# Attention and top-1 experts on one Trainium2 core: the first group's tokens are finished in their places and scattered straight to the output

## The chip, the cores and the metric

One core of a Trainium2 chip. The time is the device time of one execution in microseconds (us), the median of several runs; lower is better. The engines are TensorE (PE; its weight loads are listed apart as PEld), VectorE (DVE), ScalarE (ACT), GpSimd (POOL) and SyncE (SP), which here only issues DMA transfers. The kernel is written with a fixed order: what the code emits for an engine runs on that engine in the emitted order, and the transfers of SP's queue likewise.

## The reference

```
x = x + LN(attn(LN(x)))                     # (2, 2048, 256), 4 heads of 64
x = x + LN(ffn(LN(x)))

attn:  xn = LN(x)*gamma + beta;  q, k, v = xn @ w.T, split in heads
       q, k = rmsnorm(q, q_gamma) * 64**-0.5, rmsnorm(k, k_gamma)
       softmax(q k^T) v, heads joined, @ w_o.T + b_o

ffn:   chosen = argmax(x @ gate_w.T)        # one of 8 experts for each token
       return x + expert_w[chosen] @ x
```

All in float32. LN without gamma and beta is the plain layer norm over the 256 columns. So each token needs attention over its batch's 2048 tokens, and then one 256x256 product with the weight of the expert that the gate chose for it.

## The kernel before

**Tokens and steps.** The 4096 tokens are 32 tiles of 128, 16 to a batch. Attention is a row of 256 steps, taken two by two as 128 pairs; below, a slot is the work of one pair. For each step, `scores` makes s = K·Qᵀ on PE (L1071, for two heads and 512 queries) and ACT turns it into p = exp(s) (L1079, five buffers of p, two PSUM tiles of s); `add` sums p over the keys on DVE (L1112, L1114), `weigh` multiplies by V on PE into po (L1123). In a slot the code emits the scores of the next pair, the sums of this pair, then `between(now)`, and then the po of this pair. `between` moves every running generator on by one step: all other work (projections, tokens, gate, places) is made of generators whose steps it puts into the slots. After the last pair `finish` runs what is left, each time the step that can start first by costs written in the code.

**Tokens after attention.** When four tiles have their attention, `tokens` (L811) makes for each: py = oT·woT on PE (L817), y = py + bias (L832) with the gate's columns, the norm's moments on DVE (L387, L389), rs and shift on POOL (`norm`: rs L383, shift L400; here they are named rs_z and away), then x2 = y·scale + xr (L843), the gate's scores into the group's `picks` (L851), the moments of x2, and x2n = LN(x2) on ACT (L868). SP writes x2 (L871) and x2n (L872) to DRAM, 128 KB each.

**Groups.** Tiles 0 to 15 are group A (T=16), tiles 16 to 27 group B (T=12); the last four tiles go a dense way with all eight experts. When the last tile of a group has its scores, `choose_all` (L580, last instruction L593) finds the expert of each token on DVE, and `order` (L597) sorts the tokens by expert into S = T+7 places of 128 rows, so that each place holds tokens of one expert: two rank matmuls on PE (L603, L604), a chain of small DVE instructions that ends in each token's position `pos` (L652), then, a slot later, the place's expert, and the matrices ids (L678, L679) and inrow (L686, four 128x512 instructions), and two slots later a product on PE (src, L696, one 128x128 by S matmul for each of the T tiles) that gives for each place the list of its tokens. DVE casts it to integers (L703).

**Places.** One place begins in each slot. `places` (L717): POOL gathers the 128 rows of x2n by src (L722, into one of six row buffers), SP loads the expert's weight (L736), PE transposes the rows (pt_g, L744), ACT copies them (xT, L749), PE multiplies (pe, L754), ACT copies out (f, L764), DVE makes the moments, POOL rs_f and shift_f (L383, L400), ACT the norm (L770), and SP writes f as 128 rows of `fn` (L771).

**Collection.** When all places of a group are written, `collect` (L781) gathers for each tile its tokens' rows of fn by pos on POOL (L792), reads x2 back on SP (L800), adds both and `away` on DVE (L804) and writes the tile of the output on SP (L808). `away` is the part of x2 that was kept aside (minus the mean times the scale). For group A this comes among the last pairs of attention, 622 to 710 us, beside the tokens and the gate of group B.

The lines that decide where the source product stands:

```
            yield
            yield
            ps = ps_m(f"src{n}")
            for t in range(T):
                nc.tensor.matmul(ps[:, :S], inrow[t // QT4][:, t % QT4, :],
                    ids[:, t, :], start=(t == 0), stop=(t == T - 1))
            nc.vector.tensor_copy(gr.src, ps[:, :S])
            at = now + 1
            for j in range(S):
                at += 0.34 if at >= len(steps) // PAIR + lead else 1
```

Of the kernel before, what the change touches and what calls it, by code (L numbers as in the profile page):

```python
# [9 lines left out]
F32 = mybir.dt.float32  # L10
# [10 lines left out]
GAMMA_MAX = 5.0  # L21
RAISE = 1 / 16


@with_exitstack
def kernel(
# [95 lines left out]
    bo = const.tile([P, D], F32, tag="bo", name="bo")  # L122
    nc.gpsimd.dma_start(out=bo, in_=b_o.partition_broadcast(P))
# [51 lines left out]

    DG = D + E
# [4 lines left out]
    bias_o = const.tile([P, DG], F32, tag="bias_o", name="bias_o")  # L181

# [44 lines left out]
    def turn_outputs(w, ps, turned):  # L227
# [26 lines left out]
        for c in range(NCH):  # L254
# [6 lines left out]
            )  # L261
        nc.gpsimd.tensor_copy(bias_o[:, :D], bo)
        nc.vector.tensor_copy(bias_o[:, D:], pb[:, :E])
# [18 lines left out]
    def bounded_path():  # L282
# [55 lines left out]
        def tables():  # L338


            make_upper_triangular(nc, before, 1.0, diag=False)
            nc.gpsimd.memset(allones, 1.0)
            for r, step, per_partition in ((col, 1, 0), (col128, P, 0), (token, P, 1)):
                nc.gpsimd.iota(
                    r,
                    [[step, r.shape[-1]]],
                    base=0,
                    channel_multiplier=per_partition,
                    allow_small_or_imprecise_dtypes=True,
                )  # L350
            yield
# [179 lines left out]
        ring = []  # L531
        rows = []
        spare = []

        def more_room():

            for i in range(2):
                acc = wk.tile([P, HP, KB], F32, tag="acc", name=f"rows{i}", bufs=2)
                rows.extend(acc[:, r, i : i + D] for r in range(HP) for i in range(0, KB, D))
            p = wk.tile([P, HP, KB], F32, tag="p", name="spare", bufs=5)  # L540
            spare.extend(p[:, r, i : i + D] for r in range(HP) for i in range(0, KB, D))
            have["f"] += len(spare)
            KT = batches[-1].KT
            ring.extend(
                KT[:, c, i : i + NCH * D].rearrange("p (c d) -> p c d", d=D)
                for c in range(NCH)
                for i in range(0, N, NCH * D)
            )

        def load_experts():  # L550
# [5 lines left out]
            )  # L556
            xg = wk.tile([P, 6, D], F32, tag="rows", name="rows", bufs=1)
            rows.extend(xg[:, i, :] for i in range(6))
            weD = kv.tile([P, NCH, E, D], F32, tag="KT", name="weD")
# [4 lines left out]
        class Group:  # L564


            def __init__(self, name, n):
# [4 lines left out]
                self.pos = route.tile([P, n], U32, tag=f"pos{name}", name=f"pos{name}")  # L572
                self.src = route.tile([P, self.S], U32, tag=f"src{name}", name=f"src{name}")
                self.exp = route.tile([P, self.S], I32, tag=f"exp{name}", name=f"exp{name}")
                self.away = route.tile([P, n], F32, tag=f"away{name}", name=f"away{name}")
                rows = dict(x2=n * P, x2n=n * P, fn=self.S * P)
                for k, v in rows.items():
                    setattr(self, k, dram.tile([v, D], F32, tag=k + name, name=k + name))

# [17 lines left out]
        def order(gr):  # L597
# [53 lines left out]
            nc.vector.tensor_reduce(pos, w, AX.X, ALU.add)  # L651
            nc.vector.tensor_copy(gr.pos, pos)  # L652
            yield
# [38 lines left out]
            yield  # L692
            yield
            ps = ps_m(f"src{n}")
            for t in range(T):
# [6 lines left out]
                )  # L702
            nc.vector.tensor_copy(gr.src, ps[:, :S])  # L703

            at = now + 1
            for j in range(S):
                at += 0.34 if at >= len(steps) // PAIR + lead else 1
                g = opens(early(places(gr, j)), Next("POOL", 1.3), 0, lambda: 0.0 if ring and rows else None)
                queue.append((at, g))
            for t in range(T):  # L710
                at += 0.5 if at >= len(steps) // PAIR + lead else 1
# [4 lines left out]

        def places(gr, j):  # L717

            n = f"{gr.name}{j}"
# [29 lines left out]
            nc.scalar.copy(xT, pt[:, :D].rearrange("p (c n) -> p c n", n=P))  # L749
            rows.append(xg)  # L750
            yield later("PE", 0.9, take="mf", give="m")
            pe = ps_m(f"pe{n}")[:, :D]
# [4 lines left out]
            ring.append(w)  # L757
            f = spare.pop() if spare else None
            own = f is None
            if own:  # L760
                f = wk.tile([P, D], F32, tag="fl", name=f"f{n}", bufs=5)
            yield then("ACT", 1.5 if j % 3 == 0 else 0.4, give="x")
# [12 lines left out]
            if not own:  # L775
                spare.append(f)
            yield later("", 0.0, give="f")
# [3 lines left out]
        def collect(gr, t):  # L781

            n = f"{gr.name}{t}"
            if attending:
                z = wk.tile([P, 2 * D], F32, tag="fg", name=f"fg{n}")
            else:
                if not free:
                    qt = kv.tile([P, NCH, KB], F32, tag="QT", name=f"fg{n}", bufs=NKB + 1)
                    free.extend(qt[:, c, :] for c in range(NCH))
                z = free.pop(0)  # L790
            o, x2 = z[:, :D], z[:, D:]
# [9 lines left out]
            yield later("DVE", 0.5, 3.0)  # L801
            if attending:
                yield later("DVE", 0.5)
            nc.vector.scalar_tensor_tensor(  # L804
# [6 lines left out]
        def tokens(bt, qb, j, oTs, gr):  # L811
# [21 lines left out]
            nc.sync.dma_start(out=xr, in_=x_f[tt * P : (tt + 1) * P, :])  # L833
            if gr:
                away = gr.away[:, tt - gr.first : tt - gr.first + 1]
# [96 lines left out]

        have = dict(m=3, s=2, x=4, f=4)

# [620 lines left out]
```

## Time and profile before

| what | us |
|---|---|
| median of three runs (802.62, 804.57, 805.9) | 804.57 |
| the profiled execution | 796.33 |
| its span (first to last instruction) | 794.6 |
| PE busy | 760.0 |
| DVE / ACT / POOL busy | 607.9 / 459.6 / 323.9 |
| L792, 16 gathers of A's collection on POOL | 18.2 |
| L804, 16 adds of A's collection on DVE | 7.7 |
| L722, 23 gathers of A's places on POOL | 28.9 |
| pairs of attention with A's places among them | 495 to 600 |
| B's gate, from the last picks on | 678 on |
| end of attention | 717 |

"Span" is the profiled time on the chip; the mean granted clock of PE over it was 0.982. In the lines of the profile "out<-in" names the tiles, "x" counts, and what stands in square brackets is the idle time of the engine just before, with what ended it. The transfers of A's fn took 2.5 us from issue to landing, those of x2 1.7, of the weights (ring) 2.9, all by SP's queue.

### The profile page before, as it was taken

Reading aid. Unit: us, or ns where it says so; the run is one execution under the profiler, and the core shown is the slowest. Engines: PE = TensorE matmul, PEld = TensorE weight load, DVE = VectorE, ACT = ScalarE, POOL = GpSimd, SP = SyncE. Lnnn points to the kernel's source line nnn. Section 1 sums busy time; section 2 is a strip of 40 time slices with the busy share of each in tenths; the row PEclk is TensorE's granted clock in tenths of the full one; section 3 lists DMA queues with packets and bytes.
Section 4 is the critical chain, followed back from the end, with each engine's and each line's share of the span. In section 5 each row is a group of like instructions: output and inputs, shape, how many; then the busy total and the mean of one; then the engine's idle time right before and its main releaser. Section 6 shows DMA issues by size and latency. Waiting matters only on the chain.

```text
span 794.6 us, 10249 instructions
## 1 busy us (share of the span) xinstructions
PE 760.0 (96%) x3169; PEld 320.3 (40%) x3169; DVE 607.9 (77%) x1239; ACT 459.6 (58%) x725; POOL 323.9 (41%) x349
## 2 busy tenths in 40 slices
PE   7999999999999999999999989999999999898794
PEld 5555433433343334333333343444444333335452
DVE  3666567598886877887888986777786889996767
ACT  3766765656565566556556525566656555445861
POOL 4644311133342523432325121757663455335324
PEclk9999999999999999999999979999999999899998
DMA  4100121210110000000221040443421243358336
GB/s 129 55 27 26 41 80 40 67 34 19 35 34 7 21 21 20 21 21 20 73 81 47 27 132 14 127 132 110 112 66 34 80 120 99 124 155 255 90 114 188
DMA packets 48149, 57.57 MB, mean 72 GB/s; under 512 B 5868, under 2 KB 39416, under 8 KB 48088
## 3 DMA queue, kind: packets, MB, share of 16 engines
q1 hardware_dynamic: 41528, 44.65, 17.8%
q0 software_dynamic: 3568, 9.32, 4.7%
q10 hardware_dynamic: 2992, 2.88, 1.3%
q8 instruction: 27, 0.44, 0.3%
q14 instruction: 34, 0.28, 0.1%
HBM read 37.69 MB, written 19.14 MB: 72 GB/s over the span
## 4 chain that ended last, share of the span: by engine, by line
PE 85%; DVE 8%; ACT 3%; issue 2%; POOL 2%; DMA 1%; POOLq 0%; DVEq 0%; ACTq 0%
PE s L1071 28%; PE po L1123 27%; PE pqk L464 7%; PE pv L473 4%; PE py L817 3%; PE peA L754 3%; PE pe L893 2%; PE pt_qk L501 2%; PE sm L1087 2%; DVE acc L1114 2%; PE pt_x L451 1%; PE peB L754 1%; DVE acc L1099 1%; PE srcA L696 1%; PE pt_gA L744 1%
## 5 line engine op out<-in xcount | busy, mean ns | idle before, releaser
L1079 ACT ACTIVATE p<-s,nbound 128x1024 f32<-128x1024 f32 x256 | 271.4, 1110 | 232.2 <-PE s L1071 224.5
L1114 DVE TENSOR_TENSOR acc<-acc,p 128x1024 f32<-128x1024 f32 x224 | 273.8, 1222 | 37.0 <-ACT p L1079 25.5
L1071 PE MATMUL s<-QT,KT 64*128 64x512 f32 x1024 | 256.5, 619 | 0.4 <-ACT p L1079 0.4
L1123 PE MATMUL po<-p,V 128*64 128x512 f32 x1024 | 251.6, 613 | 0.0
L1071 PEld LDWEIGHTS s<-QT,KT 64*128 64x128 f32 x1024 | 89.0, 188 | 164.6 <-issue 96.1
L1123 PEld LDWEIGHTS po<-p,V 128*64 128x64 f32 x1024 | 64.1, 137 | 129.8 <-issue 127.3
L383 POOL TENSOR_TENSOR rs_z<-rs_t,mhalf 128x1 f32<-128x1 f32 x28 | 36.8, 1316 | 123.3 <-DVE rs_t L382 123.2
L383 POOL TENSOR_TENSOR rn<-rs_t,mhalf 128x8 f32<-128x8 f32 x32 | 58.6, 1831 | 69.3 <-DVE rs_t L382 69.3
L464 PE MATMUL pqk<-wqkT,xnT 128*128 128x512 f32 x128 | 62.4, 611 | 0.6 <-ACT xnT L455 0.6
L383 POOL TENSOR_TENSOR roots<-rs_t,mhalf 128x1 f32<-128x1 f32 x32 | 23.9, 747 | 93.3 <-DVE rs_t L382 93.1
L1099 DVE RECIPROCAL acc<-acc 128x128 f32<-128x128 f32 x60 | 56.7, 945 | 0.0
L383 POOL TENSOR_TENSOR rs_y<-rs_t,mhalf 128x1 f32<-128x1 f32 x28 | 33.7, 1204 | 35.4 <-DVE rs_t L382 32.8
L832 DVE TENSOR_TENSOR y<-py,bias_o 128x264 f32<-128x264 f32 x28 | 12.0, 430 | 41.8 <-PE py L817 41.8
L722 POOL DMA_INDIRECT rows<-x2nA,srcA x23 | 28.9, 1257 | 30.1 <-DMA ring<-weTd 24.7
L817 PE MATMUL py<-woT,oT 128*128 128x264 f32 x128 | 35.7, 402 | 3.6 <-ACT xTB L749 2.3
L792 POOL DMA_INDIRECT fgA<-fnA,posA x16 | 18.2, 1136 | 44.8 <-DMA out_dram<-fgA 10.3
L473 PE MATMUL pv<-wvT,xnT 128*128 128x264 f32 x128 | 33.7, 386 | 0.0
L487 DVE TENSOR_REDUCE ss<-sq 128x8 f32<-128x512 f32 x32 | 21.8, 680 | 14.9 <-ACT sq L484 14.9
L473 PEld LDWEIGHTS pv<-wvT,xnT 128*128 128x128 f32 x128 | 24.5, 191 | 17.8 <-issue 10.4
L817 PEld LDWEIGHTS py<-woT,oT 128*128 128x128 f32 x128 | 22.0, 189 | 18.9 <-issue 12.1
L464 PEld LDWEIGHTS pqk<-wqkT,xnT 128*128 128x128 f32 x128 | 22.3, 195 | 17.7 <-issue 16.6
L481 ACT COPY qk<-pqk 128x512 f32<-128x512 f32 x32 | 18.7, 585 | 17.6 <-PE pqk L464 17.4
(270 smaller groups left out, 882.1 us busy)
## 6 DMA issues: line engine op xcount, KB each, us to landing
ring<-weTd SPq DMA_DIRECT2D x34, 256.0 KB, 2.9
x<-in_L_attn_x_dram SPq DMA_DIRECT2D x8, 512.0 KB, 3.9
xr<-in_L_attn_x_dram SPq DMA_DIRECT2D x28, 128.0 KB, 2.3
fnA<-fA SPq DMA_DIRECT2D x23, 128.0 KB, 2.5
we_raw<-in_L_ffn_expert_w_dram ACTq DMA_DIRECT2D x8, 256.0 KB, 2.7
weTd<-weT SPq DMA_DIRECT2D x8, 256.0 KB, 2.0
x2A<-x SPq DMA_DIRECT2D x16, 128.0 KB, 1.7
fgA<-x2A SPq DMA_DIRECT2D x16, 128.0 KB, 2.0
```

Of the source, the lines that this page charges most:

```text
L383: nc.gpsimd.tensor_tensor(dst, t[:, :n], mhalf[:, :n], ALU.pow)
L464: nc.tensor.matmul(pqk, xnT[:, c, :], wqkT[:, c, :, :].rearrange("p a d -> p (a d)"), start=(c == 0), stop=(c == NCH - 1),)
L473: nc.tensor.matmul(pv[:, :DG], xnT[:, c, :], wvT[:, c, :], start=(c == 0), stop=(c == NCH - 1),)
L487: nc.vector.tensor_reduce(ss, sq.rearrange("p (g d) -> p g d", d=DH), AX.X, ALU.add)
L722: nc.gpsimd.indirect_dma_start(out=xg, out_offset=None, in_=gr.x2n[:, :], in_offset=bass.IndirectOffsetOnAxis(ap=gr.src[:, j : j + 1], axi ...
L754: nc.tensor.matmul(pe, xT[:, c, :], w[:, c, :], start=(c == 0), stop=(c == NCH - 1))
L817: nc.tensor.matmul(py, oT[:, bass.ts(j, P)], woT[:, c, :], start=(c == 0), stop=(c == NCH - 1),)
L1071: nc.tensor.matmul(s[:, r, :], bt.KT[rows, c, bass.ts(kc, P)], bt.QT[qb][rows, c, :], start=True, stop=True,)
L1079: nc.scalar.activation(p, s, AF.Exp, bias=nbound)
L1099: nc.vector.reciprocal(acc[:, 0, cols], share[:, cols])
L1114: nc.vector.tensor_tensor(acc, acc, p, ALU.add)
L1123: nc.tensor.matmul(po[r * DH : (r + 1) * DH, :], batches[b].V[:, kc, h * DH : (h + 1) * DH], p[:, r, :], start=(kc == 0), stop=(kc == NT - 1),
```

## The change

Group A becomes "direct", group B stays as it was.

- x2n of A is a matrix of 2·256 columns in DRAM: [x2n | x2 + away]. One more activation per token tile makes the right half, and one SP write of 256 KB carries both.
- The places of A gather rows of 512 columns, into seven row pairs instead of six rows. f is written into the left half of the pair, DVE adds it to the right half, and, a slot later, POOL stores the right half by an indirect DMA straight to the rows of the output. Then the pair is free again. fn of A is not written.
- The list of rows in the output, `dst`, comes from the source product: the tokens' numbers begin at −8192, so that a row of a place with no token has 8192 or more after adding and falls outside the bound; src is the same sum cut off at the last row. Two DVE instructions stand where the cast was.
- `collect` isn't run for A.
- A's source product has one `yield` more, so it and A's places come a slot later: in PE's order it stands behind the next po and scores instead of ahead of them.
- B: its row buffers are the halves of A's pairs, six of them for f.

In the emitted order each slot has on POOL: the gather of place j+7, the store of place j, rs_f and shift_f of a later place. PE's order is otherwise the same.

```diff
+NOWHERE = 8192
...
-            for r, step, per_partition in ((col, 1, 0), (col128, P, 0), (token, P, 1)):
+            for r, base, step, per_partition in (
+                (col, 0, 1, 0),
+                (col128, 0, P, 0),
+                (token, -NOWHERE, P, 1),
+            ):
...
+        ROWS = 7
         spare = []
+
+        def split_rows():
+
+            halves = [w[:, i : i + D] for w in rows for i in (0, D)]
+            assert len(halves) == 2 * ROWS, "pairs of rows are in use"
+            rows[:], spare[:] = halves[have["f"] :], halves[: have["f"]]
...
-            xg = wk.tile([P, 6, D], F32, tag="rows", name="rows", bufs=1)
-            rows.extend(xg[:, i, :] for i in range(6))
+            xg = wk.tile([P, ROWS, 2 * D], F32, tag="rows", name="rows", bufs=1)
+            rows.extend(xg[:, i, :] for i in range(ROWS))
...
-            nc.vector.tensor_copy(gr.pos, pos)
+            if not gr.direct:
+                nc.vector.tensor_copy(gr.pos, pos)
...
             yield
             yield
+            if gr is groups[0]:
+                yield
             ps = ps_m(f"src{n}")
...
-            nc.vector.tensor_copy(gr.src, ps[:, :S])
+
+            nc.vector.tensor_scalar(
+                gr.src, ps[:, :S], float(NOWHERE), float(T * P - 1), ALU.add, ALU.min
+            )
+            if gr.direct:
+                nc.vector.tensor_scalar(
+                    gr.dst, ps[:, :S], float(NOWHERE + gr.first * P), None, ALU.add
+                )
+            else:
+                split_rows()
...
-            for t in range(T):
+            for t in range(0 if gr.direct else T):
                 at += 0.5 if at >= len(steps) // PAIR + lead else 1
...
-            rows.append(xg)
-            yield later("PE", 0.9, take="mf", give="m")
+            if not gr.direct:
+                rows.append(xg)
+            yield later("PE", 0.9, take="m" if gr.direct else "mf", give="m")
...
-            f = spare.pop() if spare else None
-            own = f is None
-            if own:
-                f = wk.tile([P, D], F32, tag="fl", name=f"f{n}", bufs=5)
+            f = xg[:, :D] if gr.direct else spare.pop(0)
...
             nc.scalar.activation(f, f, AF.Identity, bias=shift, scale=scale)
+            if gr.direct:
+                yield then("DVE", 0.4)
+                nc.vector.tensor_tensor(xg[:, D:], xg[:, D:], f, ALU.add)
+                yield later("POOL", 1.3)
+                nc.gpsimd.indirect_dma_start(
+                    out=out_f,
+                    out_offset=bass.IndirectOffsetOnAxis(ap=gr.dst[:, j : j + 1], axis=0),
+                    in_=xg[:, D:],
+                    in_offset=None,
+                    bounds_check=NTT * P - 1,
+                    oob_is_err=False,
+                )
+                rows.append(xg)
+                yield later("", 0.0)
+                return
             nc.sync.dma_start(out=gr.fn[j * P : (j + 1) * P, :], in_=f)
...
             if gr:
-                x2n = wk.tile([P, D], F32, tag="x2n", name=f"x2n{tt}")
+                both = wk.tile([P, 2, D], F32, tag="x2n", name=f"x2n{tt}")
+                x2n = both[:, 0, :]
+                if gr.direct:
+                    nc.scalar.activation(both[:, 1, :], x2, AF.Identity, bias=away)
             nc.scalar.activation(x2n, x2, AF.Identity, bias=shift, scale=scale)
             if gr:
                 rows = slice((tt - gr.first) * P, (tt - gr.first + 1) * P)
-                nc.sync.dma_start(out=gr.x2[rows, :], in_=x2)
-                nc.sync.dma_start(out=gr.x2n[rows, :], in_=x2n)
+                if gr.direct:
+                    nc.sync.dma_start(
+                        out=gr.x2n[rows, :].rearrange("p (a d) -> p a d", d=D), in_=both
+                    )
+                else:
+                    nc.sync.dma_start(out=gr.x2[rows, :], in_=x2)
+                    nc.sync.dma_start(out=gr.x2n[rows, :], in_=x2n)
                 return
...
-        have = dict(m=3, s=2, x=4, f=4)
+        have = dict(m=3, s=2, x=4, f=6)
...
-            groups.append(Group(name, n))
+            groups.append(Group(name, n, direct=first == 0))
```

The rest of the diff makes the group's DRAM tensors to match (x2n of A with 512 columns, no x2, fn, pos and away for A), takes the collection's branch for running attention away, and lets b_o and the bias share one tile, which saves a copy on POOL.

More of the change, by code (lines that the diff above doesn't have):

```diff
@@ L121 @@
         nc.gpsimd.dma_start(out=g_k[r * DH : (r + 1) * DH, :], in_=k_gamma.unsqueeze(1))
-    bo = const.tile([P, D], F32, tag="bo", name="bo")
+    DG = D + E
+    bias_o = const.tile([P, DG], F32, tag="bias_o", name="bias_o")
+    bo = bias_o[:, :D]
     nc.gpsimd.dma_start(out=bo, in_=b_o.partition_broadcast(P))
@@ L172 @@
     gate_c = const.tile([E, D], F32, tag="gate_c", name="gate_c")
-    DG = D + E
     wqkT = const.tile([P, NCH, 2, D], F32, tag="wqkT", name="wqkT")
@@ L180 @@
     gateT = const.tile([P, NCH, E], F32, tag="gateT", name="gateT")
-    bias_o = const.tile([P, DG], F32, tag="bias_o", name="bias_o")
     def turn_weight(w, pt, dst, copy=nc.vector.tensor_copy):
@@ L261, in turn_outputs @@
             )
-        nc.gpsimd.tensor_copy(bias_o[:, :D], bo)
         nc.vector.tensor_copy(bias_o[:, D:], pb[:, :E])
@@ L346, in tables @@
                     [[step, r.shape[-1]]],
-                    base=0,
+                    base=base,
                     channel_multiplier=per_partition,
@@ L540, in more_room @@
             p = wk.tile([P, HP, KB], F32, tag="p", name="spare", bufs=5)
-            spare.extend(p[:, r, i : i + D] for r in range(HP) for i in range(0, KB, D))
-            have["f"] += len(spare)
+            more = [p[:, r, i : i + D] for r in range(HP) for i in range(0, KB, D)]
+            spare.extend(more)
+            have["f"] += len(more)
             KT = batches[-1].KT
@@ L564, in bounded_path, with __init__ @@
         class Group:
-            def __init__(self, name, n):
+            def __init__(self, name, n, direct):
+                self.direct = direct
                 self.name, self.T, self.S, self.met = name, n, n + E - 1, 0
@@ L571, in __init__ @@
                 self.picks = route.tile([P, n, E], F32, tag=f"picks{name}", name=f"picks{name}")
-                self.pos = route.tile([P, n], U32, tag=f"pos{name}", name=f"pos{name}")
                 self.src = route.tile([P, self.S], U32, tag=f"src{name}", name=f"src{name}")
                 self.exp = route.tile([P, self.S], I32, tag=f"exp{name}", name=f"exp{name}")
[L575 to L578, printed above, removed]
+                rows = dict(x2n=(n * P, D), x2=(n * P, D), fn=(self.S * P, D))
+                if direct:
+                    self.dst = route.tile([P, self.S], U32, tag="dst", name="dst")
+                    rows = dict(x2n=(n * P, 2 * D))
+                else:
+                    self.pos = route.tile([P, n], U32, tag="pos", name="pos")
+                    self.away = route.tile([P, n], F32, tag="away", name="away")
+                for w, shape in rows.items():
+                    setattr(self, w, dram.tile(list(shape), F32, tag=w + name, name=w + name))
         def choose_all(gr):
@@ L774, in places @@
             yield later("", 0.0, 2.5)
-            if not own:
-                spare.append(f)
+            spare.append(f)
             yield later("", 0.0, give="f")
@@ L783, in collect @@
             n = f"{gr.name}{t}"
[L784 to L790, printed above, removed]
+            if not free:
+                qt = kv.tile([P, NCH, KB], F32, tag="QT", name=f"fg{n}", bufs=NKB + 1)
+                free.extend(qt[:, c, :] for c in range(NCH))
+            z = free.pop(0)
             o, x2 = z[:, :D], z[:, D:]
@@ L801, in collect @@
             yield later("DVE", 0.5, 3.0)
-            if attending:
-                yield later("DVE", 0.5)
             nc.vector.scalar_tensor_tensor(
@@ L833, in tokens @@
             nc.sync.dma_start(out=xr, in_=x_f[tt * P : (tt + 1) * P, :])
-            if gr:
+            if gr and not gr.direct:
                 away = gr.away[:, tt - gr.first : tt - gr.first + 1]
@@ L870, in tokens @@
                 rows = slice((tt - gr.first) * P, (tt - gr.first + 1) * P)
-                nc.sync.dma_start(out=gr.x2[rows, :], in_=x2)
-                nc.sync.dma_start(out=gr.x2n[rows, :], in_=x2n)
+                if gr.direct:
+                    nc.sync.dma_start(
+                        out=gr.x2n[rows, :].rearrange("p (a d) -> p a d", d=D), in_=both
+                    )
+                else:
+                    nc.sync.dma_start(out=gr.x2[rows, :], in_=x2)
+                    nc.sync.dma_start(out=gr.x2n[rows, :], in_=x2n)
                 return
```

## The prediction

> **What bounds the kernel now.** I read the busy shares and slices first, then the windows (stretches of 3.41 us, the step in which the granted clock changes here), then the timeline by engine around the places that the change touches.
>
> ```profile
> PE 760.0 (96%) x3169; PEld 320.3 (40%) x3169; DVE 607.9 (77%) x1239; ACT 459.6 (58%) x725; POOL 323.9 (41%) x349
> PE   7999999999999999999999989999999999898794
> PEclk9999999999999999999999979999999999899998
> ```
>
> TensorE (PE) is busy for 96% of the span of 794.6 us. So time can only come from where PE waits, or where its clock is low. From 495 to 600 us, where group A's places run, PE is busy for all of 105 us; work of other engines is free there as long as it fits between. Two stretches differ: the end of A's gate at 450–475, and of B's at 670–684.
>
> ```profile
> 458.44:461.85 3.41, 1.24 (x11) 1.24 (x12) 3.31 (x9) 0.00 (x0) 0.00 (x0) 1.00 0.55 157
> 461.85:465.26 3.41, 3.41 (x18) 3.41 (x18) 3.31 (x4) 1.11 (x1) 0.00 (x0) 0.50 0.77 226
> 468.68:472.09 3.41, 3.41 (x10) 1.01 (x8) 2.35 (x2) 0.00 (x0) 2.93 (x2) 0.50 0.14 32
> 673.48:676.89 3.41, 0.48 (x4) 0.00 (x0) 2.79 (x7) 2.39 (x3) 2.96 (x4) 1.00 0.25 76
> 676.89:680.30 3.41, 1.94 (x6) 1.22 (x8) 3.10 (x10) 0.00 (x0) 2.09 (x2) 0.50 0.46 138
> 693.96:697.37 3.41, 3.41 (x28) 2.86 (x29) 3.38 (x5) 1.20 (x2) 0.00 (x0) 1.00 0.63 208
> 697.37:700.78 3.41, 3.41 (x10) 1.08 (x8) 3.27 (x7) 0.00 (x0) 1.24 (x1) 0.50 0.61 175
> ```
>
> The columns are the stretch, PE, PE's weight loads, DVE, ACT, POOL (busy us and count), granted clock, DMA. A stretch in which PE works little (1.24, 0.48), or on small matmuls alone (693.96, mostly the source product of B), is followed by one at clock 0.50. After A's gate the clock is 0.50 for three stretches, after B's for two.
>
> **Part 1: the source product of A one slot later.**
>
> ```profile
> 454.64 1.99 PE L1071 MATMUL s<-QT,KT 64*128 64x512 f32 x8
> 460.61 5.91 PE L696 MATMUL srcA<-idsA,inrowA 128*128 128x23 f32 x32 [3.98 <-DVE inrowA L686]
> 466.44 3.68 PE L1123 MATMUL po<-p,V 128*64 128x512 f32 x8
> ...
> 459.87 2.49 DVE L686 TENSOR_TENSOR inrowA<-rowA,col 128x512 f32<-128x512 f32 x4
> 462.28 2.54 DVE L1114 TENSOR_TENSOR acc<-acc,p 128x1024 f32<-128x1024 f32 x2
> ...
> 463.59 1.11 ACT L1079 ACTIVATE p<-s,nbound 128x1024 f32<-128x1024 f32 x1 [6.64 <-DVE acc L1114]
> ```
>
> Before, PE ends a pair's scores at 456.6, idles for 4 us until the tiles of inrow come, makes the source product in 5.91 us (mostly at half clock), then po in 3.68 and the next scores, and starts the following po at 473.04. The change puts that po and those scores ahead of the product. But DVE is full from 444 to 468, and its two sums of p at 462.28 stand behind the gate's chain. ACT's exp waits for the first of them (6.64 us, to 463.59), since p has five buffers. So after: po from 456.6 to 458.5 (1.94 at full clock), half of the scores to 459.5, and then the other half waits until the exp at 463.59 has read the other score tile, 464.7. PE idles for 5.2 instead of 4. The stretches 458.44 and 461.85 hold 1.0 and 0.6 us of work, so the clock is halved: scores 1.9, to 466.6; product 5.9, to 472.5. PE stands 0.5 us better than at 473.04, but its clock, back at 472.09 before, stays low to 475.5 (product out of the way when the stretch from 472.09 begins) or 478.9: half of 3.0 or of 6.4 us is lost, 1.5 or 3.2. Sum: +1.0 or +2.7; I take the middle, **+1.8 us**.
>
> **Part 2: no collection of A.** Gone are 16 gathers (L792, 1136 ns each on POOL), 16 reads of x2, 16 adds (L804, 480 ns on DVE) and 16 writes on SP. On PE nothing changes; what matters is who waits for DVE and POOL. From 651.8 to 717 DVE has no idle time but two waits of 0.45, and B's gate hangs on it:
>
> ```profile
> 669.03 0.48 DVE L804 SCALAR_TENSOR_TENSOR fgA<-fgA,awayA 128x256 f32<-128x256 f32 x1
> 669.96 0.48 DVE L843 SCALAR_TENSOR_TENSOR x<-y,rs_z,xr 128x256 f32<-128x256 f32 x1 [0.45 <-POOL rs_z L383]
> ...
> 666.52 1.09 POOL L792 DMA_INDIRECT fgA<-fnA,posA  x1 [3.19 <-DVE mv_z L389]
> ...
> 678.36 0.74 PE L603 MATMUL rankB<-picksB,before 128*128 128x96 f32 x2 [4.39 <-DVE picksB L593]
> ```
>
> Four of A's adds (656.68, 663.44, 669.03, 675.10) lie ahead of B's picks; each delays the next instruction by about 0.40 (0.48 less overlap): 1.6 us. The two waits for rs_z, late on POOL behind a gather of 1.09, are 0.9. So the picks, and rankB, come 2.5 us earlier, at 675.9. PE's idle time falls from 4.39 to 1.9, and the stretch 673.48 holds 0.5+1.0 = 1.5 us of work instead of 0.48. That lies between 1.24 (halved next) and two stretches, 455.02 with 1.60 and 741.74 with 1.81, that were not. I take it as not halved (about 8 in 10). Then rank 0.7, po 1.94 and scores 1.94 end at 680.4 instead of 685.36 (at half clock): **−5.0 us**; with the clock halved all the same, −2.5. DVE follows: six more adds (681 to 709) give it −2.4 beyond the −2.5, −4.9 by 717, so it takes nothing back. B's source product and its half-clock stretch (697.37) stay in both.
>
> The Trainium skill bears on both parts: "TensorE: Matmul & The Clock Gate", section "Why this matters for your kernels", has it that gaps of PE above some 3 us between bursts bring the clock down. By that rule the 1.9 us left at B would not halve the clock, as I took it; but it names idle time only, while the trace halved the clock after 693.96, busy for all of 3.41 us. By the idle rule alone A's product would cost no clock, and part 1 would be only −0.5.
>
> **Part 3: what is added, and its cover.** (a) A second activation (L868's kind, 599 ns) for each of 16 tokens, 9.6 us of ACT between 184 and 451, where ACT is busy 55–66%: nothing, because PE waits there for 1 us in all; without that cover 9.6. (b) 16 writes of 256 KB on SP's queue instead of 32 of 128 KB, and 23 fewer for fn: fewer issues on SP, so nothing is pushed later there. The gather fetches 2 KB rows: nearest rows land in 3.2 (gather) and 2.9 us (256 KB, ring), against a lead of 10 to 13 us between a gather and its transposes: nothing. (c) 23 DVE adds of 0.45 in 495–600, where DVE is busy 80.7 of 105: 10.4 into 24.3 idle, nothing. A chain of add then store follows L770, which nothing on PE waits for until the row pair is used again, seven places on. (d) 23 stores on POOL, in order, each between the next gather and the norm of the next place:
>
> ```profile
> 495.00:600.00 105.00, 105.00 (x460) 45.75 (x460) 80.72 (x165) 66.64 (x108) 70.00 (x78) 1.00 0.37 105
> ...
> 504.59 1.99 POOL L722 DMA_INDIRECT rows<-x2nA,srcA  x1 [0.17 <-issue]
> ...
> 509.13 1.09 POOL L722 DMA_INDIRECT rows<-x2nA,srcA  x1 [0.17 <-issue]
> ```
>
> A slot takes 5.4 us of PE (19.4 in 105); POOL is busy 70.0/19.4 = 3.6 of it, so 1.8 are left. No row shows an indirect store. The nearest, L722, is 1.09 at its median and 2.03 at its longest; with a gap of 0.2 to 0.3 the store takes 1.3 to 2.3. It cannot gain, since nothing is taken from POOL there. I take 1.3, the median, which fits: 0. The next gather also waits for the store of a slot before to land; behind it on POOL stand that slot's store and rs_f and shift_f, for which ACT's L770 waits. At the median landing of 3.2 the loop is 1.1 + 0.3 + 3.2 = 4.6, with rs_f and shift_f (0.73 + 0.53) inside the wait: under 5.4.
>
> The 1.99 beside DVE's sums of p, against 1.09 without, is a row that speaks against (d). The Trainium skill's "SBUF — State Buffer", section "Who interferes with whom", says that descriptors written by GpSimd starve while DVE holds the shared port, and gives 620 ns growing to 3100; by that figure, an estimate, the store would be up to 3.4 us, and the lag 1.6 a slot.
>
> **Sum.** −5.0 + 1.8 = −3.2 us: the profiled execution of 796.33 (span 794.6 and 1.7 around it) becomes 793.1, span 791.4. That execution is 8.2 under the median of 804.57; I carry the difference over: **801.4 us**. With the bounds of parts 1 and 2 (+1.0 to +2.7, −5.0 to −2.5) and 1 us to each side, its own range is 799 to 806.
>
> **Rivals.**
> 1. The move hides the wait. If the exp came in time, po and the scores (1.94 + 1.99) would fill the 4.0 us of idle time: −4.0; they would run at full clock, −2.7 (3.68 + 2.9 against 3.9); the product would too, 3.7 instead of 5.91, −2.2; one stretch of half clock follows it, +1.7. Sum −7.2 in place of +1.8: 804.57 − 7.2 − 5.0 = 792.4. For it: po needs only p that is there. Against: the exp's 6.64 us wait for DVE, unchanged. 0.13.
> 2. POOL becomes the bound in 495–600, slower. It decides once a store with its gap and with exposed landing costs over 1.8 us a slot. At 2.03 + 0.3 the slot is 5.9: a lag of 0.55 × 19 = 10.4, less the 6 of slack that the lead leaves, +4; with −3.2, 805.4. If the wait for the landing lies open, at the longest landing of L722's rows (5.5), the loop is 1.1 + 0.3 + 5.5 = 6.9: a lag of 24 to 33 and, less slack and with −3.2, 820 to 826. Between them 811. For it: 1.99 beside DVE's sums, and POOL in order, with every gather tied to a store. Against: POOL's idle third. 0.27.
> 3. B's clock is halved anyway, so the removal yields only 2.5: −0.7, 803.9. For it: 1.5 is nearer to 1.24 than to 1.81. Against: 1.60 passed. 0.05, since the forecast's range holds most of it.
>
> **Chances.** 0.5% (4 us) is about what a measurement of this kernel can tell from no change: under 800.55 is faster, over 808.6 slower. The forecast (0.55) splits into 0.26 faster, 0.27 same, 0.02 slower; rival 1 is faster (0.13); rival 2 slower 0.24, same 0.03; rival 3 same (0.05). Faster 0.39, same 0.35, slower 0.26. The range 793 to 813 leaves out half of rival 1 and the upper 0.11 of rival 2.
>
> **What would show it.** Part 1: an idle of about 5 us ahead of the second half of the scores, ended by the exp, and the clock low for four stretches from about 461.9. Part 2: rankB's wait under 2.5 us and no half clock after it. Part 3: PE without waits for pt_gA and peA, stores of about 1.1 us. It is wrong if the transposes pt_gA wait for gathers, if L722 waits for a landing for long, or if the source product's wait is gone.

## The result and the profile after

The changed kernel takes 807.91 us (median of 11 runs, 805.25 to 808.93) against 804.57 before (11 runs, 802.3 to 806.22): ratio 1.0044, 95% interval 1.003 to 1.0058. It is slower by 3.3 us; a gain of 3.2 was forecast. The profiled execution has a span of 806.8 us.

The busy shares and slices of the changed kernel, as shown of before:

```profile
PE 766.8 (95%) x3169; PEld 324.3 (40%) x3169; DVE 610.0 (76%) x1246; ACT 466.7 (58%) x741; POOL 332.1 (41%) x355
...
PE   7999999999999999999999799999989999996993
...
PEclk9999999999999999999999969999999999999697
```

The slices of PE no longer show B's gate, but have an 8 three quarters of the way to the end, where before had only nines: that is among A's places. To say where the 12.2 us between the two profiled spans arise, one needs marks that both kernels have. ACT's 256 exps are such marks (exp 0 to exp 255, in order, two to a slot); their start times, read out of the two traces, give the stages:

```
                              before    changed   difference
start to exp 4                 56.44     55.11      -1.33
exp 4 to 156                  399.40    399.40       0
156 to 164 (A's product)       28.69     31.22      +2.53
164 to 216 (A's places)       136.91    142.59      +5.68
216 to 240                     51.72     51.72       0
240 to 255 (B's gate)          40.41     35.21      -5.20
exp 255 to the end             81.00     91.57     +10.57
```

The stages in the middle agree to a hundredth where nothing was changed. The start differs by one stretch of half clock that fell into it before (45.4 to 48.8). The end differs by half clock too: while PE still worked there was none of it before and 17.1 us after (735.7 to 739.1 and 746.0 to 759.6). Is the end a part of the change? The profiled execution of before (796.33) was 8.2 us under its median and under all eleven timed runs, that of the changed kernel (808.59) 0.7 over its median, so much of the 10.6 need not belong to the change; experiments 1 and 5 look at this.

**A's product.** The timeline of PE and ACT of the changed kernel, start and duration first:

```profile
455.23 1.94 PE L1172 MATMUL po<-p,V 128*64 128x512 f32 x8
457.10 1.13 PE L1120 MATMUL s<-QT,KT 64*128 64x512 f32 x4
463.25 2.08 PE L1120 MATMUL s<-QT,KT 64*128 64x512 f32 x4 [5.02 <-ACT p L1128]
465.26 7.02 PE L720 MATMUL srcA<-idsA,inrowA 128*128 128x23 f32 x32
...
462.08 1.11 ACT L1128 ACTIVATE p<-s,nbound 128x1024 f32<-128x1024 f32 x1 [6.45 <-DVE acc L1163]
```

PE's wait has only moved: 5.02 us ahead of the second half of the scores, ended by an exp that had itself waited 6.45 us for DVE's sum. Then the product takes 7.02 at half clock.

**B's gate.** PE at B's rank matmuls:

```profile
682.53 0.46 PE L624 MATMUL rankB<-picksB,before 128*128 128x96 f32 x2 [1.68 <-DVE picksB L614]
```

The wait is 1.68 us, where it was 4.39, and the matmuls run at full clock (0.46 for what took 0.74).

**A's places.** Here are the lines that were not forecast. First PE and ACT, then POOL, all of the changed kernel:

```profile
595.71 2.02 PE L789 MATMUL peA<-ring,xTA 128*128 128x256 f32 x4 [2.25 <-ACT xTA L783]
...
594.52 0.60 ACT L802 ACTIVATE rows<-rows,shift_fA,rs_fA 128x256 f32<-128x256 f32 x1 [4.23 <-POOL shift_fA L405]
595.03 0.35 ACT L796 COPY rows<-peA 128x256 f32<-128x256 f32 x1
595.28 0.37 ACT L783 COPY xTA<-pt_gA 128x256 f32<-128x256 f32 x1
...
592.38:595.79 3.41, 1.16 (x7) 0.28 (x3) 2.58 (x4) 1.27 (x4) 3.05 (x4) 1.00 0.46 136
595.79:599.20 3.41, 3.41 (x10) 2.00 (x12) 3.27 (x7) 1.89 (x2) 2.78 (x4) 0.50 0.27 80
```

Read it backwards: PE waits for xT; the copy that makes xT is third in a row on ACT, behind the norm of an earlier place (L802), though the transposes that it copies had ended at 589.67; and the norm waits 4.23 us for shift_f on POOL. The stretch in which PE waits has 1.16 us of work, and the next one runs at clock 0.50. PE's three waits of this kind in the stage (0.24, 0.96 and 2.25) and half of the 3.41 us at half clock make 5.2 of the 5.7 us.

```profile
573.37 1.04 POOL L807 DMA_INDIRECT out_dram<-rows,dst  x1 [0.31 <-issue]
574.45 0.59 POOL L388 TENSOR_TENSOR rs_fA<-rs_t,mhalf 128x1 f32<-128x1 f32 x1
575.13 0.27 POOL L405 TENSOR_SCALAR shift_fA<-mv_fA,rs_fA 128x1 f32<-128x1 f32 x1
577.96 1.08 POOL L756 DMA_INDIRECT rows<-x2nA,srcA  x1 [2.56 <-DMA out_dram<-rows,dst]
579.34 1.11 POOL L807 DMA_INDIRECT out_dram<-rows,dst  x1 [0.30 <-issue]
580.47 0.77 POOL L388 TENSOR_TENSOR rs_fA<-rs_t,mhalf 128x1 f32<-128x1 f32 x1
```

POOL itself stands still for 2.56 us, with a gather at its head that waits for the store of the slot before to land. (In the trace the gather of place j+6 and, behind it, the store of place j stand in one slot; the gather of place j+7, which takes the pair of place j, comes a slot later.) Eight other gathers of A wait for over a microsecond and are put down to ACT or PE, but the packets of the stores in the trace tell the same of all nine: the gather begins 1.14 to 1.33 us after the last packet. Five of them:

```
store issued   its last packet   next gather begins
549.34         552.68            553.87
556.27         558.61            559.83
566.71         570.20            571.34
573.37         576.62            577.96
579.34         581.66            582.87
```

From a store's issue to the next gather's start it is 3.5 to 4.6 us in these nine (mean 4.1). Gathers follow each other every 5.96 us (mean of 15 intervals), where PE's slot is 5.4. The mean has two parts. Seven intervals hold a token's rs and shift on POOL beside the place's, and take 6.3 us; the other eight hold less work but wait for a landing, and take 5.7, so they can't make good what the seven lose.

### The profile page after: what moved, and what is told of

Its sections match the earlier page's. It is cut to its first block, busy times and chain, and to the rows that moved or that the text cites. A ratio compares the mean times of both kernels' runs of the same rounds, so it can differ in the third digit from the quotient of the medians.

```text
span 806.8 us, 10130 instructions
## 1 busy us (share of the span) xinstructions
PE 766.8 (95%) x3169; PEld 324.3 (40%) x3169; DVE 610.0 (76%) x1246; ACT 466.7 (58%) x741; POOL 332.1 (41%) x355
## 4 chain that ended last, share of the span: by engine, by line
PE 78%; DVE 9%; issue 4%; ACT 3%; POOL 2%; DMA 2%; another core or an unknown queue 0%; SPq 0%; POOLq 0%; DVEq 0%; ACTq 0%
PE s L1120 25%; PE po L1172 25%; PE pqk L469 7%; PE pv L478 4%; PE py L858 4%; PE peA L789 2%; DVE acc L1163 2%; PE pt_qk L506 2%; PE pe L942 2%; PE sm L1136 2%; PE peB L789 1%; PE pt_x L456 1%; POOL rows L756 1%; DMA x<-in_L_attn_x_dram 1%; DMA out_dram<-rows,dst 1%
## 5 line engine op out<-in xcount | busy, mean ns | idle before, releaser
L388 POOL TENSOR_TENSOR rs_z<-rs_t,mhalf 128x1 f32<-128x1 f32 x28 | 38.9, 1390 | 113.4 <-DVE rs_t L387 113.3
L388 POOL TENSOR_TENSOR rs_y<-rs_t,mhalf 128x1 f32<-128x1 f32 x28 | 31.0, 1107 | 44.1 <-DVE rs_t L387 42.5
L756 POOL DMA_INDIRECT rows<-x2nB,srcB x19 | 21.2, 1114 | 22.5 <-DMA ring<-weTd 17.0
L789 PE MATMUL peA<-ring,xTA 128*128 128x256 f32 x92 | 26.9, 416 | 3.7 <-ACT xTA L783 3.5
L942 PE MATMUL pe<-weD,kept 128*128 128x512 f32 x64 | 29.8, 624 | 0.0
L805 DVE TENSOR_TENSOR rows<-rows 128x256 f32<-128x256 f32 x23 | 9.8, 427 | 26.3 <-ACT rows L802 26.2
```

The source lines that it names most:

```text
L388: nc.gpsimd.tensor_tensor(dst, t[:, :n], mhalf[:, :n], ALU.pow)
L756: nc.gpsimd.indirect_dma_start(out=xg, out_offset=None, in_=gr.x2n[:, :], in_offset=bass.IndirectOffsetOnAxis(ap=gr.src[:, j : j + 1], axi ...
L789: nc.tensor.matmul(pe, xT[:, c, :], w[:, c, :], start=(c == 0), stop=(c == NCH - 1))
L942: nc.tensor.matmul(pes[:, r].rearrange("p e d -> p (e d)"), xT[:, c, :], weD[:, c, e + r * EB : e + (r + 1) * EB, :].rearrange("p e d -> p ...
```

## The experiments

All ratios are to the kernel before, run in turn with the experiment on the same chip. These chips ran the kernel before at a median of 796.5 to 799 us instead of 804.6, so times are to be compared within a group only; the times expected in 1 to 4 start from 804.6 and are compared as ratios. The medians scatter: in 1 the same kernel has 796.42 and 799.02 at a ratio of 0.9989, so the ratio, with its interval, can differ from the quotient of two medians by 0.2%. The stages by exps, of each profiled execution (us):

```
                              156-164  164-216  216-240  240-255   end   ratio
1  before, again                28.68   136.91    51.72    40.28  84.22  0.9989
5  changed, again               31.82   142.98    51.72    35.13  86.11  1.0055
2  eighth pair                  32.06   138.52    51.72    33.49  82.69  0.9995
3  product back                 28.46   142.29    51.72    35.15  83.78  1.0001
4  before, product later        32.04   136.91    51.72    40.49  82.95  1.0076
6  eighth pair, product back    28.48   136.91    51.72    36.79  84.66  0.9946
7  gather last                  31.75   139.67    51.72    35.14  83.93  1.0016
8  before, no collection of A   28.69   136.91    51.72    36.79  84.00  0.9949
9  as 6, stores twice           28.49   183.91    51.82    35.49  86.62  1.0561
11 as 6, more work on POOL      29.45   154.60    52.19    33.83  85.42  1.0175
10 as 6, chain spread           20.43   138.53    55.34    35.13  81.49  0.9876
12 before, chain spread         18.93   138.53    55.33    39.45  94.52  1.0114
```

**1 and 5. Both kernels once more.** No edit.

> The kernel before, unchanged, as a yardstick and for a second profile. Theory: between the two profiles at hand the changed kernel loses 2.5 us at A's source product and 5.7 among A's places and gains 5.25 at B's gate, and the other 9 us of the difference (start, and the tail after the last exp: 85.8 us before, 96.3 after) are chance of the profiled execution; then this profile's tail is well above 85.8 (90 to 96) with the same order and its time 802 to 806. Rival: the tail is really slower after the change; then this tail is about 86 again.

> The changed kernel, unchanged, beside the others on one chip. Theory: from exp to exp nothing but chance changes: +2.5 to +3.4 us against before from exp 156 to 164, +5.7 to 216, -5.2 from 240 to 255, and a tail like that of before on this chip (within 2 us): 3 us slower, ratio 1.003 to 1.005. Rival: the tail of the changed kernel, 91.6 us in its profile, is its own: then it is over 88 here beside one of about 84 of before, and the ratio is 1.008 or more.

Measured: before 0.9989 (0.997 to 1.0008) to itself; the changed kernel 1.0055 (1.0032 to 1.0078). The expectation of 1 counts the tail from exp 252, where 81.0 and 91.6 are 85.8 and 96.4; so counted this profile of before has 89.0, between the theory (90 to 96) and the rival (about 86). From exp 255 the end of before is 84.22, that of the changed kernel 86.11 instead of 91.57. So a large part of the 10.6 came from the two executions that were profiled; 1.9 us are left between the kernels, less than between two executions of one kernel (81.0 and 84.2, 91.6 and 86.1), and the changed kernel with a part undone (2, 3, 7) has 82.7 to 83.9. The three stages that were changed repeat: +3.1, +6.1, −5.2, together +4.1, and the timed medians differ by 4.0 (802.91 against 798.91).

**2. The wait for the landing.** An eighth row pair, so that a gather takes the pair of the store two slots back:

```diff
+        eighth = []
...
             if gr.direct:
+                eighth.append(wk.tile([P, 2 * D], F32, tag="qk", name="row8", bufs=4))
+                rows.extend(eighth)
```

The rest of the edit keeps the eighth pair out of the halves that B gets.

> The changed kernel with an eighth row pair for A's places, so that a gather takes the pair of the store two slots back and not of the one just before it. Theory: the gather's wait for that store to land (3.5 to 4.6 us from issue, then 1.2) makes the slot 6.0 us instead of 5.4, and rs_f and shift_f behind it come late; without it the 5.7 us between pairs 92 and 108 fall to at most 1: 802 to 803.5. Rival: the 23 stores' own time on POOL (1.35 each with their gap) is the bound; then the loss stays, 807 to 808.5, with POOL still without idle time around 545 to 600.

Measured: 797.07 against 799.02, ratio 0.9995 (0.9976 to 1.0014). From 804.57 the theory's times are ratios of 0.997 to 0.999 and the rival's 1.003 to 1.005, which the interval leaves out. The places lose 1.6 us instead of 5.7 to 6.1. So the landing made over 4 us of the loss. (The 3.5 to 4.6 us of the expectation already hold its 1.2.) The 1.6 is more than the 1 expected: gathers follow at 5.65 us (mean of 15), and none has POOL idle before it for longer than 0.52 us. The intervals with a token's work take 6.6 us (6.3 in the changed kernel), and the others, now without a wait, 4.8 instead of 5.7. Gathers without and with a token's work between them:

```profile
573.96 1.08 POOL L760 DMA_INDIRECT rows<-x2nA,srcA  x1 [0.52 <-issue]
579.16 1.08 POOL L760 DMA_INDIRECT rows<-x2nA,srcA  x1 [0.17 <-issue]
586.17 1.08 POOL L760 DMA_INDIRECT rows<-x2nA,srcA  x1 [0.17 <-issue]
593.03 1.09 POOL L760 DMA_INDIRECT rows<-x2nA,srcA  x1 [0.52 <-ACT p L1132]
597.71 1.08 POOL L760 DMA_INDIRECT rows<-x2nA,srcA  x1 [0.52 <-PE s L1124]
```

That POOL's own work makes the 1.6 left is inferred from this.

**3. The product back.**

```diff
             yield
             yield
-            if gr is groups[0]:
-                yield
             ps = ps_m(f"src{n}")
```

> The changed kernel without the additional yield: A's source product again ahead of po and scores. Theory: the move cost 2.5 us, since the second half of the scores waits for an exp that waits for DVE's sums; undone, 805.0 to 806.0, and PE waits about 4 us ahead of the product instead of 5 ahead of the scores. Rival: the difference at this place is only where the clock's stretches fall; then 807 to 808.5.

Measured: ratio 1.0001 (0.9981 to 1.0021), with 28.46 us at A's product against 31.22 and 31.82 with the move; PE waits 3.79 us ahead of the product:

```profile
458.78 6.67 PE L718 MATMUL srcA<-idsA,inrowA 128*128 128x23 f32 x32 [3.79 <-DVE inrowA L708]
```

The places begin a slot earlier and take 142.29 us, where the changed kernel took 142.59 and 142.98. The move cost 2.8 to 3.4 us in its stage. The rival's ratio, 1.003 to 1.005, lies outside the interval.

**4. Only the move, in the kernel before.**

```diff
             yield
             yield
+            if gr is groups[0]:
+                yield
             ps = ps_m(f"src{n}")
```

> The kernel before with only the source product of A one slot later. Theory: 2.5 us slower, 806.5 to 807.6, with a wait of about 5 us for the exp. Rival: no change at this place, 804 to 805.2.

Measured: 803.65 against 799.02, ratio 1.0076 (1.0048 to 1.0104): 6 us by the ratio, 4.6 by the medians, of which the stage shows 3.4 (PE waits 5.22 us for the exp, then 17 us at half clock).

```profile
463.03 2.08 PE L1073 MATMUL s<-QT,KT 64*128 64x512 f32 x4 [5.22 <-ACT p L1081]
465.04 7.02 PE L698 MATMUL srcA<-idsA,inrowA 128*128 128x23 f32 x32
```

The profiled execution is 3.6 under the run's median, and where the timed runs lost the remainder was not seen. That is more than the 2.5 expected; the direction is clear, and nothing else in the stages moved.

**6. Both undone together.** The edits of 2 and 3.

> The changed kernel with both undone: an eighth row pair, and the source product back ahead of po and scores. Theory (the parts add): 0 from exp 156 to 164, +1.6 to 216, -5.2 to 255 or -6.9 where the clock is not halved after B's product: 3.6 to 5.3 us faster than before, ratio 0.993 to 0.9955. Rival: with the product back the places begin a slot earlier and POOL lags all the more, so the loss to 216 stays at 5: ratio 0.999 to 1.001.

Measured: 794.49, ratio 0.9946 (0.9925 to 0.9967), faster than both kernels. The places lose nothing at all (136.91), which is better than the 1.6 that were expected to stay. With the product back they begin a slot earlier, which may be the reason; with seven pairs (3) a slot earlier alone was worth 0.3 to 0.7 us. The windows of the same 105 us in the changed kernel and in this one:

```profile
495.00:600.00 105.00, 101.31 (x436) 43.80 (x434) 81.24 (x168) 61.62 (x98) 78.25 (x86) 0.98 0.38 119
```

```profile
495.00:600.00 105.00, 105.00 (x459) 45.28 (x460) 86.34 (x180) 65.35 (x107) 86.34 (x94) 1.00 0.40 123
```

POOL is the fifth pair of figures. It is busy for 78.25 us in the kernel where it holds PE up, and 86.34 in the one where it does not: a busy share would have named the wrong kernel. What counted were the waits between.

**7. Another order instead of another buffer.** Seven pairs; the gather last in its slot:

```diff
-                g = opens(early(places(gr, j)), Next("POOL", 1.3), 0, lambda: 0.0 if ring and rows else None)
+                pl = places(gr, j)
+                g = opens(pl if gr.direct else early(pl), Next("POOL", 1.3), 0, lambda: 0.0 if ring and rows else None)
```

> The changed kernel with each gather of A's places emitted at the end of its slot, behind the store, rs_f and shift_f, instead of ahead of them, with seven pairs. Theory: the landing that a gather waits for is a store of the slot before, and now nothing of the same slot stands behind that wait; the loss from exp 164 to 216 falls from 5.7 to 0.5 to 2. Rival: POOL has too much to do in any order: 4 to 6 stays.

Measured: ratio 1.0016 (0.9994 to 1.0038); the places lose 2.8 us, between the two expectations (0.5 to 2, and 4 to 6). The wait for xT is gone, and a new one has come: the rows themselves are late.

```profile
596.18 0.44 PE L779 MATMUL pt_gA<-ident,rows 128*128 128x128 f32 x2 [1.47 <-DMA rows<-x2nA,srcA]
```

**8. Collection alone.** The kernel before, with the collection of A left out, so the first 2048 rows of the output are not written:

```diff
-            for t in range(T):
+            for t in range(0 if gr is groups[0] else T):
                 at += 0.5 if at >= len(steps) // PAIR + lead else 1
```

> The kernel before without the collection of group A; the rows of A's output are not written. Theory: A's sixteen gathers and adds alone delay B's gate; without them exp 240 to 255 takes 5.2 us less and nothing else moves: ratio 0.9935. Rival: part of the 5.2 came from elsewhere (the transfers and stores of the places that are over by then): then 2 to 4 us less.

Measured: 793.99, ratio 0.9949 (0.9928 to 0.9969), 3.5 us less from exp 240 to 255 and nothing elsewhere: by its size a hit for the rival. But PE's wait for the picks is 1.66 us, as after the change (1.68); only, here the clock was halved for one stretch after it, which makes the difference to 5.2. The wait and the windows around it in this kernel, and the one in the changed kernel, which no half clock followed:

```profile
674.53 0.46 PE L603 MATMUL rankB<-picksB,before 128*128 128x96 f32 x2 [1.66 <-DVE picksB L593]
```

```profile
671.93:675.34 3.41, 1.75 (x12) 0.83 (x10) 3.13 (x13) 2.60 (x3) 0.49 (x1) 1.00 0.23 77
675.34:678.75 3.41, 3.41 (x10) 0.63 (x7) 3.20 (x9) 0.03 (x1) 2.35 (x2) 0.50 0.11 38
```

```profile
681.14:684.55 3.41, 2.02 (x12) 1.01 (x12) 3.10 (x10) 1.51 (x3) 1.18 (x1) 1.00 0.34 115
```

With the same wait, half clock followed on 1.75 us of work in the stretch, and not on 2.02. So 3.5 us, from the wait itself and the shorter half clock, are collection's, and the 1.7 up to 5.2 hang on where the stretch begins: 6, which has A's stores, has 36.79 and the half clock too. The rival's source (transfers and stores) is not needed.

**9. Stores twice.** The edit of 6, and the store's call repeated.

> The kernel of e6_pair_and_product with each of the 23 stores of A issued twice. Theory: in e6 POOL is busy 86.3 of the 105 us from 495 to 600, 4.45 a slot of 5.4, and with the gaps ahead of gathers and stores (some 0.7) about 5.2; a second store with its gap, 1.35, makes 6.5, so POOL lags by 1.1 a slot for 19 slots, and less a slack of 6 the exps 164 to 216 take 10 to 20 us more. Rival: what costs time is only the wait for a landing, and POOL's own work is hidden: then at most 2 us more.

Measured: 842.81, ratio 1.0561 (1.0519 to 1.0602); the places take 47 us more. That is over twice what was expected, and for another reason: the second store waits for the first to land, presumably since it writes the same rows of the output.

```profile
545.28 1.03 POOL L809 DMA_INDIRECT out_dram<-rows,dst  x1 [0.30 <-issue]
548.98 1.85 POOL L817 DMA_INDIRECT out_dram<-rows,dst  x1 [2.67 <-DMA out_dram<-rows,dst]
```

The run did not tell POOL's work from a wait, but it prices one more store with its landing on POOL's path: 2.5 us a slot over 19.

**11. POOL's work alone.** The edit of 6, and behind each store:

```diff
+                for _ in range(2):
+                    more = small.tile([P, 1], F32, tag="more", name=f"more{n}", bufs=1)
+                    nc.gpsimd.tensor_tensor(more, half, mhalf[:, :1], ALU.pow)
```

> The kernel of e6_pair_and_product with two small POOL instructions more behind each of A's 23 stores (the same kind as rs, 0.58 to 1.5 us each, that wait for no transfer). The second stores of e9 each waited 1.7 to 2.9 us for the first to land, so that run did not show POOL's own work alone; this one does. Theory: work alone also decides, once a slot is over 5.4: 4.45 + 0.7 + 1.4 to 2.5 = 6.5 to 7.6, exps 164 to 216 10 to 25 us longer than the 136.9 of e6. Rival: only waits for landings make POOL late: at most 2 us longer.

Measured: 811.21, ratio 1.0175 (1.0145 to 1.0206); the places take 17.7 us more, and PE waits for xT behind ACT ten times by 0.2 to 2.5 us. No gather waits over 0.52. So work without any landing decides too, once a slot is full. One of the waits, with the norm on ACT behind it that waits for POOL:

```profile
551.26 0.60 ACT L804 ACTIVATE rows<-rows,shift_fA,rs_fA 128x256 f32<-128x256 f32 x1 [4.50 <-POOL shift_fA L405]
...
552.44 1.13 PE L791 MATMUL peA<-ring,xTA 128*128 128x256 f32 x4 [2.52 <-ACT xTA L785]
```

**10 and 12. The chain of A's gate spread.** In A's product PE waits because DVE is late, wherever the product stands. The edit, on the kernel of 6 (10) and, with `gr is groups[0]` for `gr.direct`, on the kernel before (12), puts five yields into `order`, so that the chain comes in pieces:

```diff
+            if gr.direct:
+                yield
             over = wk.tile([P, E, NT], F32, tag="over", name=f"over{n}", bufs=1)[:, :, :T]
...
+            if gr.direct:
+                yield
             ge = wk.tile([P, NT, NT + E], F32, tag="ge", name=f"ge{n}", bufs=1)[:, :T, : S + 1]
...
+            if gr.direct:
+                yield
             row = small.tile([P, NT], F32, tag="row", name=f"row{n}", bufs=1)[:, :T]
...
             for t in range(0, T, QT4):
+                if gr.direct and t % (2 * QT4) == 0:
+                    yield
```

> The kernel of e6_pair_and_product with A's chain on DVE cut into pieces of 0.8 to 1.2 us in five more slots, the source product in the slot after the last. Theory: PE's wait at A's gate is DVE's lag (the chain stands ahead of the sums of p, and p has five buffers), not the place of the product; spread, the lag is made good from slot to slot, the wait of 3.8 is gone, and of three stretches of half clock one stays: 5 to 8 us less than e6, 786.5 to 789.5 by a before of 798.9, ratio 0.984 to 0.988. Rival: the sums of the following slots fill DVE in any case and the wait only comes elsewhere, or the later places run into B's gate: ratio 0.993 to 0.997.

> The kernel before, with its collection, and only A's chain on DVE spread as in e10. Theory: the spread is worth the same without the direct stores at A's gate (6 us from exp 156 to 168), and since collection comes five slots later it takes some of B's gate with it or leaves for the end: ratio 0.990 to 0.997, slower than e10. Rival: the direct stores bring nothing beside it: ratio 0.986 to 0.989 as e10.

Measured for 10: 788.39 against 798.51, ratio 0.9876 (0.9841 to 0.9911), the fastest of all. The product comes later and at full clock, without a wait of its own:

```profile
469.46 1.93 PE L1146 MATMUL sm<-acc,ones 128*64 128x512 f32 x4 [2.51 <-DVE acc L1173]
...
479.58 3.75 PE L728 MATMUL srcA<-idsA,inrowA 128*128 128x23 f32 x32
```

One wait of 2.51 for DVE is left, and two stretches of half clock instead of three. Against 6 the stages from exp 156 to 240 take 2.8 us less together (214.3 for 217.1): the places take 1.6 more, as they also do in 12 without any store, and the stage behind them 3.6. Another 1.7 at B's gate is the half clock that did not follow there, and 3.2 lie in the end.

Measured for 12: 805.62 against 796.47, ratio 1.0114 (1.009 to 1.0138): slower, outside both expectations. A's gate gains as in 10 (4.5 us from exp 156 to 240 together), but collection, five slots later, now stands between B's gathers on POOL, and the end takes 94.52 us instead of 84.22:

```profile
711.68 1.51 POOL L800 DMA_INDIRECT fgA<-fnA,posA  x1 [1.54 <-DVE fgA L812]
713.50 1.03 POOL L730 DMA_INDIRECT rows<-x2nB,srcB  x1 [0.31 <-DMA out_dram<-fgA]
...
726.09 0.66 PE L752 MATMUL pt_gB<-ident,rows 128*128 128x128 f32 x2 [4.54 <-DMA rows<-x2nB,srcB]
```

## Why the prediction was wrong

**Part 1, the product (+1.8 forecast): right, and a little small.** The exp that waits for DVE's sum, the wait of about 5 us ahead of the second half of the scores (5.02) and the half clock after it came as written. It cost 2.5, and 3.1 to 3.4 in other executions, because the clock stayed low for four or five stretches and the product took 7.0 us instead of 5.9: the 5.91 had begun at full clock. Experiments 3 and 4 show it as the move's own cost.

**Part 2, collection (−5.0): right.** Wait 1.68 (1.9 forecast), no half clock, −5.2. Experiment 8 shows the shorter wait as collection's own. That the clock might be halved all the same was rightly kept open: it was in 6 and 8, with −3.5 (−2.5 forecast for that case). So the last 1.7 of the 5.2 were partly luck.

**Part 3, (a) to (c): no trace of a cost.** The stage from exp 4 to 156 is the same to 0.01 us, with the 16 more activations in it; and in experiment 6 the stage from exp 164 to 216, with the wider gathers and the 23 adds in it, takes the 136.91 of before.

**Part 3 (d), the stores (0): the step that failed.** It was written: "At the median landing of 3.2 the loop is 1.1 + 0.3 + 3.2 = 4.6, with rs_f and shift_f (0.73 + 0.53) inside the wait: under 5.4." The store's own price was right, 1.04 at its median against 1.3 taken with its gap (1.04 + 0.30). What was mis-sized is the landing as the next gather feels it: 3.5 to 4.6 from the store's issue where POOL waits for it, 4.1 in the mean, so that the loop is 5.5 (1.1 + 0.3 + 4.1) and not 4.6. The 3.2 was a gather's median, taken since no store was to be seen. And the sum was made for one mean slot: in slots with a token's rs and shift POOL was busy for longer (6.3 from gather to gather), and the loop of the other slots left no time to catch up. The mean came to 5.96, over the 5.4 from which rival 2 decides; rival 2's bounds (5.9 and 6.9) held it, and the effect, 5.7 to 6.1 us, is near its lower end (4 net of slack). The upper end of rival 2's sum is 828 by its own terms (33 less 6 and 3.2 over 804.57), not 826. Experiment 2 shows that the landing is the larger part of the cause, and 11 that POOL's work alone can cost as well; that it is the part left in 2 is inferred. The price by the Trainium skill's "SBUF — State Buffer", a store of up to 3.4, was not met: the longest store here took 1.94, beside DVE's sums. That page's figure is for a DVE copy, and it stands in the section "A bandwidth-pool intuition that's wrong (but worth ruling out)".

A second thing was left out, in (c) and (d) together. They say that L770 waits for shift_f, and that nothing on PE waits for L770. But ACT worked in the emitted order (594.52, 595.03, 595.28 above), and behind L770 stand the copies that make xT for the next place; PE reached the late POOL through them.

**The sum.** +1.8 − 5.0 + 0 should have been +2.5 − 5.2 + 5.7 = +3.0; the timed medians gave +3.3. Carrying the difference to the median held here and in 5 (4.1 by the stages, 4.0 by the medians), but not in 4, where the timed runs lost 1.2 to 2.7 us more than the stage shows; comparing the profiled ends (81.0 and 91.6) would have misled.

## What to carry to other kernels

When a buffer is given back by a transfer, ask which instruction waits for the landing and what is queued behind that instruction on its engine; here one more buffer was worth over 4 of the 5.7 to 6.1 us lost, and together with a slot earlier all of it. Price a loop that holds a landing from issue to the waiter's start, add what the engine has to do besides, and follow a late engine through in-order neighbours until it meets the one that counts. A wait that comes from a lagging engine isn't removed by moving the waiting instruction (2.5 to 3.4 us lost): spread the lagging engine's work (in experiment 10 the best version, 1.2% faster than before).

## What the runs showed of the hardware that was not expected

- An indirect store of 128 rows of 1 KB takes POOL 1.04 us (median of 23; 1.94 at the longest), its last packet is seen 1.8 to 3.9 us after issue, and the nine gathers on POOL that waited for one began 1.14 to 1.33 us after that packet.
- The same wait of PE, 1.66 to 1.68 us, halved the clock for a stretch in two kernels, where it left 1.75 us of work in one stretch of 3.41, and did not in the changed kernel, where it left 2.02. Before had stretches with 1.60 and 1.81 that were not followed by half clock, so the busy time alone doesn't decide it. The rule that the prediction cites from the Trainium skill ("TensorE: Matmul & The Clock Gate", section "Why this matters for your kernels"), idle gaps above some 3 us, doesn't either: 1.66 us were followed by half clock.
- The same kernel before ran at a median of 804.6 us in one group and of 796.5 to 799 in the others. Its two profiles, at 796.3 and 797.8 us, agree to 0.02 us in every stage from exp 4 to 240 and differ at the start (1.6), at B's gate (0.1) and in the end (3.2). No profile of it at 804.6 is at hand, so where those 6 to 8 us lie was not seen.
